# Gate rows fetched into 64 of 128 partitions and copied to the other 64 by ScalarE, in a one-core MetaFormer layer

## The chip, the cores and the metric

The kernel runs on one core of one Trainium2 chip. The metric is the device time of one execution in microseconds (us). A core has TensorE (PE in the profile; PEld is its weight load), VectorE (DVE), ScalarE (ACT), GpSimd (POOL) and SyncE (SP), each with its own instruction queue that is worked off in order; SP here only issues DMAs.

## The reference: what is computed

Input `x` is 2 x 128 x 256 x 256 float32 (batch, channels, rows, columns). All arithmetic is float32.

```
x = x + attention(norm_over_channels(x))        # 8x8 windows, 4 heads, keys and values from 12x12 with a
                                                # mask that keeps positions of the query's own parity
t = tokens(x)                                   # 131072 tokens of 128 channels
h = norm(t)
p = softmax(h @ router_w + router_b)            # 8 experts; the best two kept, renormalised
t = t + sum over the two kept experts of p_e * (h @ expert_w[e] + expert_b[e])
```

Only the second half matters for the change. Each token has eight gate values (six of them zero), a mean and a rate (one over its standard deviation).

## The kernel before

**Work and order.** The image is cut into 64 strips of 8 rows, and a strip into four *planes* by the parity of row and column (the mask lets a query see its own parity only). The loop at L979 runs over 256 planes, each with 512 query positions. In the same iteration the kernel also works on one *row pair* (2 x 256 = 512 tokens) of an earlier strip for the experts. The order of the instructions of every engine is written out by hand (`manual_schedule`, L978): generators (`scores`, `attend`, `project`, `norms`, `route`, `out_project`) are advanced with `next`, so the place of a `next` or a call in the loop is the place of its instructions in the queues.

**One iteration on PE**, in order: position scores (L437), key scores (L454), the next plane's values (L310), position terms (L369), keys (L383) and queries (L408), expert products 4, 6, 7, 5 of the earlier row pair (L677), softmax sums (L475), attention times values (L485), channel sums for the norms (L543), expert products 0, 1, 2 of the next row pair (L677), output projection (L513), product 3 (L677). A matmul of the program stands as two matmul records and two weight loads in the profile.

**The gates.** For a row pair `f` and a row `c` that attention will need, `norms` (L526) makes channel sums on PE; DVE transposes them into `plg` (L552) and works out variances (L192 to L195); ScalarE takes a logarithm and an exponential (L196, L197); DVE goes on with L198. In the next iteration `route` (L569) makes the gates on DVE (L576 to L608). `spread` (L611) transposes gates, means and rates (L614) and writes them to a DRAM tile `gd`, one 512-long row per expert, one for the means (row 8) and one for the rates (row 9). Each such row is then read back by one DMA that repeats it on all 128 partitions:

- `Experts.fetch(e)` (L643) loads gate row `e` into a tile `gb` of 128 x 512. The pool has eight of them. A one-column write by DVE (L651) or ScalarE (L649) stands before the DMA (L652), so that the DMA goes out when that engine has come to this point.
- `fetch_means` (L654) loads the means into `sb` (L657), `fetch_rstd` (L625) the rates into `rb` (L628).
- `means` (L659) makes `xs = x + sb` on DVE (L662; the row holds the standard deviation minus the mean, the former carrying the bias); `times(e)` (L664) makes `xe = xs * gb` on DVE for e = 0, 1, 2, 3, 4, 6 and on POOL for 5 and 7 (L668), where a small copy (L672) holds POOL until DVE has made `xe` 6. `ln1` (L234) multiplies a row of `x` by `rb` on POOL (L236) for the attention norm.

All these DMAs are issued by SP, in the order of the calls, with the loads of `x` (`xt`, L117), the stores of the output (L715), the value rows written to DRAM (`vrows`, L329) and the value windows read back from there (`vwin`, L341).

**ScalarE in one iteration**, in order: the exponential of the router (L581), the exponential of the scores (L462), the values to SBUF (L318), the keys (L394, L404) and queries (L410) to SBUF, two squares (L537), a touch of `xt` (L116), then L196 and L197; the touches for gates 4, 5 and 7 (L649) lie between.

**The instruction stream of PE.** At the start of an iteration with n > 6 a padding instruction (L994) moves the next PE instruction to slot 157 of a block of 256 instruction slots (`BLOCK` = 256, `FIRST_LIMIT` = 99: 99 slots are left in the block). With 64 slots for L437 and two for each record of L454, the block ends at the 18th of the 128 records of L454; 256 slots later is the fourth record of the first L677, and 256 after that the 108th of 128 records of L485. `row_at` (L886) gives the row `c`; it is None for the last seven planes (249 to 255), and such an iteration has 16 matmul records fewer. There `late` (L992) adds a second padding to slot 40 (L1026) ahead of L475.

**The start.** In planes 0 to 5 (`filling`, FILL = 6) no experts are due; `norms` gets a PSUM tile of the experts for its sums (L1034), but takes `plg` from the pool of three PSUM tiles `mm` that `pv`, `pu`, `pk`, `pq` and `po` use in turn.

Of the kernel before, what the change touches and what calls it, by code (L numbers as in the profile page):

```python
# [19 lines left out]
E = 8  # L20
# [32 lines left out]
def kernel(  # L53
# [472 lines left out]
    def norms(f, c, nm, plt=None):  # L526

        g = gboth[next(g_turn) % len(gboth)]
        srcs = []
        for j, src in ((0, f and rows_of(*f)), (2, c and ln1_src(*c))):
            if src is None:
                continue
            sq = work.tile([P, CH], F32, tag=f"sq{j}", name=f"sq{j}{nm}", bufs=1)
            nc.scalar.activation(sq, src, AF.Square)  # L537
            srcs += [(j, src), (j + 1, sq)]
        yield
        plt = plt or mm_tile(f"plt{nm}")  # L540
        for j, src in srcs:
            for t in range(NT):
                nc.tensor.matmul(  # L543
                    plt[32 * t : 32 * t + 32, :P],
                    lhsT=rw[:, j],
                    rhs=src[:, t * P : (t + 1) * P],
                    start=(j == srcs[0][0]),
                    stop=(j == srcs[-1][0]),
                )
        yield  # L550
        plg = mm_tile(f"plg{nm}")
        nc.vector.transpose(plg[:, :P], plt[:, :P])  # L552
        p4 = plg[:, :P].rearrange("p (t e) -> p t e", e=32)
        k0, k1 = (0 if f else 1), (2 if c else 1)
        r, u = rstd(p4, plg[:, P : P + 2 * NT], k0, k1, nm)
        rs = None
        if f:
            rs = small.tile([P, NT], F32, tag="rs", name=f"rs{nm}")
            nc.vector.scalar_tensor_tensor(rs, u[:, 0], 3.0, r[:, 0], ALU.add, ALU.mult)
        if c:  # L560
            nc.vector.scalar_tensor_tensor(
                g[:, 1, :, 1], u[:, 1 - k0], 3.0, r[:, 1 - k0], ALU.add, ALU.mult
            )
        yield g, rs, p4
# [60 lines left out]
    def fetch_rstd(gd, nm):  # L625

        rb = gates.tile([P, NT * P], F32, tag="rb", name=f"rb{nm}", bufs=2)
        nc.sync.dma_start(rb, to_all(gd, E + 1))  # L628
        return rb

    def to_all(gd, j):

        return gd[j * NT : (j + 1) * NT].rearrange("r k -> (r k)").partition_broadcast(P)

    class Experts:

# [6 lines left out]
        def fetch(self, e, eng):  # L643


            nm = "_".join(str(v) for v in (*self.at, e))
            self.gb[e] = gates.tile([P, NT * P], F32, tag="gb", name=f"gb{nm}", bufs=8)
            if eng is nc.scalar:
                eng.copy(self.gb[e][:, 0:1], onesm[:, 0:1])  # L649
            else:  # L650
                eng.memset(self.gb[e][:, 0:1], 0.0)  # L651
            nc.sync.dma_start(self.gb[e], to_all(self.gd, e))  # L652

        def fetch_means(self):  # L654

            self.sb = gates.tile([P, NT * P], F32, tag="sb", name="sb%d_%d" % self.at, bufs=1)
            nc.sync.dma_start(self.sb, to_all(self.gd, E))  # L657

        def means(self):  # L659

# [24 lines left out]

    class NoExperts:
        def fetch(self, e, eng):
            pass

        def fetch_means(self):  # L690
# [31 lines left out]
    def finish_last(ex, nxt, gated):  # L722
# [65 lines left out]
        nxt.means()  # L788
        ex.end()
        for e in (0, 1, 2, 3, 4, 6, 5, 7):  # L790
            nxt.times(e, nc.vector)
        for e in (0, 1, 2, 3, 4, 6, 5, 7):
            nxt.product(e)
# [57 lines left out]
        for r in range(4):  # L851
# [6 lines left out]
        store(*to_store.pop())  # L858

        fetch_into(  # L860
            2, gds[1], [gates.tile([P, CH], F32, tag="gb", name=f"gl2_{e}", bufs=8) for e in range(E)]
        )

        accs = []
# [113 lines left out]
    with tc.manual_schedule(engines={ET.PE, ET.DVE, ET.Activation, ET.Pool, ET.SP}):  # L978
        for n in range(n_planes):  # L979
# [9 lines left out]

            late = n == 6 or n > 6 and row_at(n - 1) is None  # L992
            if n > 6 and (not late or row_at(n - 2) is not None):
                nc.tensor.addr_align(BLOCK, offset=BLOCK - FIRST_LIMIT)  # L994


# [8 lines left out]
            next(score, None)  # L1005
            next(ahead, None)
            nxt.fetch(7, nc.scalar)
            if gated:
                f, c, made = gated
                gd = spread(f, c, made[0], f"_{n}")  # L1010
                new = Experts(*f, gd) if f else new
# [16 lines left out]

            f = (i - 1, pl) if 0 < i <= len(strips) else None
            c = row_at(n)  # L1030
            if f or c:
                room = None
                if filling:
                    room = ps_acc.tile([P, 512], F32, tag="acc", name=f"plt_{n}")  # L1034
                norm = norms(f, c, f"_{n}", room)
            next(norm, None)
            next(attn, None)
            nxt.means()
            new.fetch_means()
            if n + 1 < n_planes:  # L1040
                take_values(n + 1)
            for e in (0, 1, 2, 3):
                nxt.times(e, dve)
            new.fetch(0, dve)
            for e in (4, 6):
                nxt.times(e, dve)
            new.fetch(1, dve)
            ex.end()
            new.fetch(2, dve)
            next(attn, None)  # L1050
# [94 lines left out]
```

## Time and profile before

| | us |
|---|---|
| median of 3 runs | 4280.03 (4274.47 to 4294.36) |
| the profiled execution | 4275.43 |
| its span, first to last instruction | 4273.6 |
| PE busy | 4202.6 (98%) |
| DVE busy | 3785.9 (89%) |
| ACT busy | 1316.4 (31%) |
| POOL busy | 1072.7 (25%) |
| DMA traffic | 1022.15 MB, 239 GB/s on the mean |

How to read the profile: the page gives busy time per engine, DMA traffic per queue, the chain of work that ended last, and groups of instructions by source line with their mean duration. The timeline lists one engine's instructions in order of time: start, duration, engine, line, operation, tiles, shape, count; in square brackets the idle time of the engine before the row and what ended it. "issue" there means that nothing in the profile explains the wait. The view of waits sums the same idle times by who waited for whom: us in total, times, longest. The view of windows gives busy us per engine for a stretch of time, then the granted PE clock, the share of the 16 DMA engines that was busy, and GB/s. "In plane" times below count from the first L437 matmul of an iteration.

### The profile page before, as it was taken

The numbers are of one execution on the slowest core, as the hardware profiler recorded it, in microseconds if no ns is written. First come the engines' busy times: TensorE is split into PE (matmuls) and PEld (weight loads), VectorE is DVE, ScalarE is ACT, GpSimd is POOL, SyncE is SP. The second block draws the span as 40 slices with busy tenths as digits, with TensorE's granted clock in tenths as the row PEclk, the third lists the DMA queues.
The fourth block names the chain that finished last, engine by engine and source line by source line (L and its number), as shares of the span: only waits on it lengthen the run. The fifth ranks groups of instructions, "written<-read, shape, count | busy, mean of one in ns | idle before, by whom it ended". The sixth has DMA issues, their size and how long they took to land.

```text
span 4273.6 us, 224029 instructions
## 1 busy us (share of the span) xinstructions
PE 4202.6 (98%) x94273; PEld 2454.3 (57%) x94273; DVE 3785.9 (89%) x11768; ACT 1316.4 (31%) x3750; POOL 1072.7 (25%) x1109
## 2 busy tenths in 40 slices
PE   7999999999999999999999999999999999999998
PEld 5555555555555555555555555555555555555554
DVE  5898889899888899998989988898989899888888
ACT  3323232323333333333333333232323233323220
POOL 1222222222222222222222222222222222222220
PEclk9999999999999999999999999999999999999999
DMA  4777778787878787887777877788777878787776
GB/s 136 233 243 243 241 244 241 246 245 243 247 237 249 236 247 241 250 240 245 246 245 239 248 241 245 237 249 241 246 242 243 243 245 250 235 239 244 238 223 218
DMA packets 824576, 1022.15 MB, mean 239 GB/s; under 512 B 137634, under 2 KB 409634, under 8 KB 823594
## 3 DMA queue, kind: packets, MB, share of 16 engines
q1 hardware_dynamic: 822864, 1007.52, 76.3%
q8 instruction: 769, 12.60, 1.3%
q14 instruction: 213, 1.74, 0.1%
q10 hardware_dynamic: 730, 0.29, 0.0%
HBM read 863.78 MB, written 143.75 MB: 236 GB/s over the span
## 4 chain that ended last, share of the span: by engine, by line
PE 97%; issue 1%; DVE 1%; DMA 0%; SPq 0%; ACT 0%; DVEq 0%
PE acc L677 41%; PE att L454 8%; PE att L485 7%; PE pv L310 7%; PE plt L543 6%; PE pu L369 5%; PE po L513 5%; PE pk L383 5%; PE pq L408 5%; PE att L437 4%; PE att L475 3%; PE accl L765 0%; DMA gl<-gd_l 0%; DVE xe L668 0%; PE pltn L253 0%
## 5 line engine op out<-in xcount | busy, mean ns | idle before, releaser
L677 PE MATMUL acc<-xe,ew 128*128 128x512 f32 x4016 | 1875.4, 599 | 4.3 <-issue 3.6
L677 PEld LDWEIGHTS acc<-xe,ew 128*128 128x128 f32 x4016 | 741.0, 189 | 900.6 <-issue 849.9
L668 DVE TENSOR_TENSOR xe<-xs,gb 128x512 f32<-128x512 f32 x1508 | 932.4, 685 | 8.6
L672 POOL COPY last<-xe 128x1 f32<-128x1 f32 x250 | 46.5, 186 | 3030.0 <-DVE gb L651 3030.0
L668 POOL TENSOR_TENSOR xe<-xs,gb 128x512 f32<-128x512 f32 x500 | 637.3, 1275 | 1.5 <-PE att L485 1.0
L454 PE MATMUL att<-qs,kcol 32*60 32x32 f32 x32768 | 393.1, 222 | 21.6 <-issue 21.3
L454 PEld LDWEIGHTS att<-qs,kcol 32*60 32x60 f32 x32768 | 387.5, 126 | 26.0 <-issue 25.2
L236 POOL TENSOR_TENSOR xn<-xt,rb 128x512 f32<-128x512 f32 x249 | 374.6, 1505 | 83.6 <-DMA rb<-gd 83.1
L485 PEld LDWEIGHTS att<-pT,vwin 64*32 64x32 f32 x32768 | 351.2, 105 | 49.8 <-issue 12.0
L485 PE MATMUL att<-pT,vwin 64*32 64x32 f32 x32768 | 349.8, 201 | 9.2 <-issue 7.9
L462 ACT ACTIVATE pT<-att 128x1024 f32<-128x1024 f32 x256 | 262.3, 1024 | 265.6 <-PE att L454 265.5
L310 PE MATMUL pv<-wt,xn 128*128 128x128 f32 x2048 | 298.2, 289 | 0.0
L537 ACT ACTIVATE sq<-xt 128x512 f32<-128x512 f32 x501 | 290.1, 630 | 0.0
L357 DVE STREAM_TRANSPOSE au<-auT 128x512 f32<-128x512 f32 x256 | 269.6, 1053 | 8.8
L394 ACT COPY kcol<-pk 128x560 f32<-128x560 f32 (+2 forms) x344 | 183.1, 532 | 290.5 <-PE pk L383 287.7
L373 DVE STREAM_TRANSPOSE uT<-pu 128x512 f32<-128x512 f32 x256 | 183.3, 716 | 96.7 <-PE pu L369 92.3
L513 PE MATMUL po<-o,wt 128*128 128x512 f32 x512 | 262.0, 593 | 4.7 <-ACT kcol L404 2.1
L383 PE MATMUL pk<-xn,wt 128*128 128x512 f32 (+2 forms) x528 | 263.6, 583 | 0.0
L369 PE MATMUL pu<-xn,wrel 128*128 128x512 f32 x512 | 263.3, 596 | 0.0
L408 PE MATMUL pq<-xn,wt 128*128 128x512 f32 x512 | 262.5, 594 | 0.5 <-issue 0.5
L310 PEld LDWEIGHTS pv<-wt,xn 128*128 128x128 f32 x2048 | 249.3, 192 | 10.6 <-DVE xn L236 0.2
L437 PEld LDWEIGHTS att<-au,keys 32*64 32x64 f32 x8192 | 115.8, 131 | 197.1 <-PE po L513 188.5
(2444 smaller groups left out, 4913.5 us busy)
## 6 DMA issues: line engine op xcount, KB each, us to landing
gb<-gd SPq DMA_DIRECT2D x2008, 256.0 KB, 5.7
vwin<-vrows SPq DMA_DIRECT2D x512, 240.0 KB, 4.9
xt<-in_x_dram SPq DMA_DIRECT2D x256, 256.0 KB, 6.6
out_dram<-xt SPq DMA_DIRECT2D x256, 256.0 KB, 6.1
sb<-gd SPq DMA_DIRECT2D x251, 256.0 KB, 4.4
rb<-gd SPq DMA_DIRECT2D x249, 256.0 KB, 3.4
vrows<-vr SPq DMA_DIRECT2D x168, 256.0 KB, 3.6
vrows<-vr SPq DMA_DIRECT2D x160, 128.0 KB, 3.5
```

What stands on the lines that cost most here:

```text
L236: eng.tensor_tensor(xn[i % 2][:, :, :, k, 1 : PC + 1], ln1_src(i, k).rearrange("p (y j x) -> p y x j", y=2, x=2), rb.rearrange("p (y j x) ...
L310: nc.tensor.matmul(pv[:, j * P : (j + 1) * P], lhsT=xp[:, k, 1 : PC + 1], rhs=wv, start=True, stop=True,)
L369: nc.tensor.matmul(pu, lhsT=wrel, rhs=inner, start=True, stop=True)
L383: nc.tensor.matmul(pk[:, : m * PC], lhsT=wk, rhs=xp[:, part[0] : part[0] + m, 1 : PC + 1], start=True, stop=True,)
L408: nc.tensor.matmul(pq, lhsT=wq, rhs=inner, start=True, stop=True)
L437: nc.tensor.matmul(sc[rows, h].rearrange("p (t w z) -> p t w z", w=2, z=16)[:, :, w], lhsT=keys[hp, turn, w], rhs=au[hp, half * NP + w : ( ...
L454: nc.tensor.matmul(sc[rows, h, 32 * t : 32 * t + 32], lhsT=kk[hp, half * HP + t, 0:NK], rhs=qs[hp, m0 : m0 + 2].rearrange("p m a s -> p (m ...
L485: nc.tensor.matmul(av[hp, half, 32 * t : 32 * t + 32], lhsT=vv[rows, t, hp], rhs=pT[rows, h, 32 * t : 32 * t + 32], start=True, stop=True,)
L513: nc.tensor.matmul(po, lhsT=wo, rhs=state["o"].rearrange("p f z -> p (f z)"), start=True, stop=True)
L537: nc.scalar.activation(sq, src, AF.Square)
L668: eng.tensor_tensor(self.xe[e], self.xs, self.gb.pop(e), ALU.mult)
L677: nc.tensor.matmul(self.acc, lhsT=ew[:, e, :], rhs=self.xe.pop(e), start=(e == 0), stop=not self.xe)
```

## The change

1. `fetch`, `fetch_means` and `fetch_rstd` load a row into 64 partitions only: the lower half for an even row number, the upper half for an odd one. A ScalarE copy (`other_half`) then fills the other 64. There are ten such copies in an iteration, at fixed places in ScalarE's order: gate 2 after the values (L318); gates 3, 4, 6 after the queries (L410), ahead of the two squares; means, gate 5, rates, gate 7 and the next row pair's gate 0 between the touch of `xt` (L116) and L196; gate 1 after L197.
2. Ten `gb` tiles instead of eight, and the loads of the next row pair's gates 0 and 1 are issued right after the means, ahead of the `vwin` reads on SP and ahead of the `times` on DVE, where before they stood behind `vwin` and between the `times`.
3. In planes 0 to 5, `plg` takes the other half of the tile that the sums are in, and no tile of `mm`.
4. The conditions for the two paddings of the PE stream are shifted by one plane. They differ from before in planes 249 and 250 alone: 249 now gets the second padding too, 250 loses the first.
5. In `finish_last` the copies stand before the `times` of the row pair that is under way; the loads of the last five row pairs stay at 128 partitions.

```diff
+        room = plt
         plt = plt or mm_tile(f"plt{nm}")
...
-        plg = mm_tile(f"plg{nm}")
+        plg = mm_tile(f"plg{nm}") if room is None else room[:, 2 * P :]
...
-        nc.sync.dma_start(rb, to_all(gd, E + 1))
+        fetch_half(rb, gd, E + 1)
...
+    def to_all(gd, j, count=P):
+        return gd[j * NT : (j + 1) * NT].rearrange("r k -> (r k)").partition_broadcast(count)
+    def halves_of(tile_, j):
+        return (tile_[0:SLOT], tile_[SLOT:])[:: 1 - 2 * (j % 2)]
+    def fetch_half(tile_, gd, j):
+        nc.sync.dma_start(halves_of(tile_, j)[0], to_all(gd, j, SLOT))
+    def other_half(tile_, j):
+        there, other = halves_of(tile_, j)
+        nc.scalar.copy(other, there)
...
-            self.gb[e] = gates.tile([P, NT * P], F32, tag="gb", name=f"gb{nm}", bufs=8)
+            self.gb[e] = gates.tile([P, NT * P], F32, tag="gb", name=f"gb{nm}", bufs=10)
...
-            nc.sync.dma_start(self.gb[e], to_all(self.gd, e))
+            fetch_half(self.gb[e], self.gd, e)
+        def double(self, e):
+            other_half(self.gb[e], e)
...
-            nc.sync.dma_start(self.sb, to_all(self.gd, E))
+            fetch_half(self.sb, self.gd, E)
+        def double_means(self):
+            other_half(self.sb, E)
...
         for e in (0, 1, 2, 3, 4, 6, 5, 7):
+            if e > 1:
+                nxt.double(e)
             nxt.times(e, nc.vector)
...
-            late = n == 6 or n > 6 and row_at(n - 1) is None
-            if n > 6 and (not late or row_at(n - 2) is not None):
+            late = n == 6 or n > 6 and row_at(n) is None
+            if n > 6 and row_at(n - 1) is not None:
                 nc.tensor.addr_align(BLOCK, offset=BLOCK - FIRST_LIMIT)
...
             nxt.fetch(7, nc.scalar)
+            nxt.double(2)
...
             c = row_at(n)
+            for e in (3, 4, 6):
+                nxt.double(e)
...
             new.fetch_means()
+            new.fetch(0, dve)
+            new.fetch(1, dve)
             if n + 1 < n_planes:
                 take_values(n + 1)
-            for e in (0, 1, 2, 3):
+            for e in (0, 1, 2, 3, 4, 6):
                 nxt.times(e, dve)
-            new.fetch(0, dve)
-            for e in (4, 6):
-                nxt.times(e, dve)
-            new.fetch(1, dve)
             ex.end()
...
             new.fetch(3, dve)
+            new.double_means()
+            nxt.double(5)
+            if row:
+                other_half(row[2], E + 1)
+            nxt.double(7)
+            new.double(0)
...
             ex.product(2)
+            new.double(1)
             new.fetch(4, nc.scalar)
```

More of the change, by code (lines that the diff above doesn't have):

```diff
@@ L627, in fetch_rstd @@
         rb = gates.tile([P, NT * P], F32, tag="rb", name=f"rb{nm}", bufs=2)
-        nc.sync.dma_start(rb, to_all(gd, E + 1))
+        fetch_half(rb, gd, E + 1)
         return rb
-    def to_all(gd, j):
-        return gd[j * NT : (j + 1) * NT].rearrange("r k -> (r k)").partition_broadcast(P)
+    def to_all(gd, j, count=P):
[7 more added lines that the diff above has]
+        nc.scalar.copy(other, there)
     class Experts:
@@ L687, in fetch, with double, double_means @@
         def fetch(self, e, eng):
+            pass
+        def double(self, e):
+            pass
+        def double_means(self):
             pass
@@ L860, in finish_last @@
         fetch_into(
-            2, gds[1], [gates.tile([P, CH], F32, tag="gb", name=f"gl2_{e}", bufs=8) for e in range(E)]
+            2, gds[1], [gates.tile([P, CH], F32, tag="gb", name=f"gl2_{e}", bufs=10) for e in range(E)]
         )
```

## The prediction

> **What bounds the kernel now.** First the page: busy time and queues.
>
> ```profile
> PE 4202.6 (98%) x94273; PEld 2454.3 (57%) x94273; DVE 3785.9 (89%) x11768; ACT 1316.4 (31%) x3750; POOL 1072.7 (25%) x1109
> ...
> q1 hardware_dynamic: 822864, 1007.52, 76.3%
> q8 instruction: 769, 12.60, 1.3%
> ```
>
> PE is the bound, and DVE is close behind. q8 moved 769 packets in 256 planes, three for each: 12.60 MB / 769 = 16.4 KB, one block of 256 instruction slots. So PE's program arrives by DMA, beside 1007 MB of data.
>
> Then I took the start of every plane (its first L437) from the timeline. Of the 246 planes from 8 to 253, 141 take 16.24 us to within 0.03; the rest are longer, by 43.8 us in sum. 16.24 is a floor: in such a plane PE is never idle. I looked in the long planes for the difference, line by line. The timeline of PE in planes 230 and 135:
>
> ```profile
> 3778.90 0.36 PE L454 MATMUL att<-qs,kcol 32*60 32x32 f32 x17
> 3780.46 1.31 PE L454 MATMUL att<-qs,kcol 32*60 32x32 f32 x111 [1.20 <-issue]
> ...
> 2226.54 1.45 PE L677 MATMUL acc<-xe,ew 128*128 128x512 f32 x3
> 2228.81 2.31 PE L677 MATMUL acc<-xe,ew 128*128 128x512 f32 x5 [0.82 <-issue]
> ...
> 2231.50 1.16 PE L485 MATMUL att<-pT,vwin 64*32 64x32 f32 x107
> 2232.83 0.32 PE L485 MATMUL att<-pT,vwin 64*32 64x32 f32 x21 [0.17 <-issue]
> ```
>
> The breaks come after 17 records of L454, 3 of L677 and 107 of L485, and no semaphore ends them: these are the three block ends of the layout that L994 makes. Summed over planes 8 to 253 (time of each group of records above its usual one): L454 24.1 us in 48 planes, first L677 8.0 in 20, L485 9.8 in 37; 41.9 in all. I set the q8 packets beside them. A break follows when the packet ends less than about 1.5 us ahead of the block end; without a break it was 1.3 to 4.0 us ahead at L454. The start of that packet in its plane varies from 11.4 to 15.5 us, so it waits its turn among the data.
>
> What it waits behind shows the view of windows, plane 60 in three stretches (0 to 3.5, 3.5 to 12, 12 to 16.25 in plane):
>
> ```profile
> 992.16:995.66 3.50, 3.50 (x171) 3.22 (x171) 3.11 (x16) 1.72 (x4) 0.00 (x0) 1.00 0.92 330
> 995.66:1004.16 8.50, 8.50 (x191) 4.71 (x190) 8.13 (x20) 2.83 (x8) 1.46 (x3) 1.00 0.66 202
> 1004.16:1008.41 4.25, 4.25 (x11) 1.58 (x10) 3.52 (x15) 0.47 (x3) 2.65 (x2) 1.00 0.82 279
> ```
>
> The last two columns are DMA share and GB/s: the DMA engines are nearly full from 12 us to the next plane's 3.5. Over 145 undisturbed planes, 14 to 16 of the 16 are busy there.
>
> **The change, part by part.**
>
> *Half loads.* 2008 + 251 + 249 = 2508 loads of 256 KB, 657 of 1007 MB, are halved: 329 MB less, a third. By the records a 2 KB packet takes 101 ns on the mean; 2508 x 64 fewer on 16 engines are 1.01 ms, so the DMA share goes from 0.76 to about 0.52. Gates 0 and 1 also leave the crowded stretch (issued at 10.8 and 11.3 in plane) for the idle one near 8. I set a backlog for each issue from these times: 0.81 us of work per 256 KB, 0.93 for a `vwin`. Before, it stands at 2 to 2.7 us from 11 to 16; after, at 0.4 to 1.4. Packets for L454 and L677 then start 1 to 2 us earlier, and their breaks should nearly all go. L485's packet starts at 6.1 to 8.2 behind gate 7, `vrows` and `gd`, of which only the first is halved; I leave 3 us there and 1 elsewhere. Bounds: nothing goes (0), all goes (-41.9). I take **-38**, nearer to the full end, because breaks are the tail of the packets' distribution.
>
> [...]
>
> *Ten copies on ScalarE.* The trace has no 64x512 copy from SBUF to SBUF. Nearest: the pair of L537 squares, same length from SBUF, 1.15 us for two, the second starting about 0.52 after the first; alone 0.63. I take 0.52 each in a row; bounds 0.18 (the one-column copy L649) and 0.65 (L394, 128x560): 5.2 us in a plane, ACT from 31% to about 62%. What counts is the queue behind them:
>
> ```profile
> 998.34 1.15 ACT L537 ACTIVATE sq<-xt 128x512 f32<-128x512 f32 x2
> 999.39 0.18 ACT L116 COPY xt<-onesm 128x1 f32<-128x1 f32 x1
> 1006.69 0.18 ACT L196 ACTIVATE r__60_19346<-plg 128x8 f32<-128x8 f32 x1 [7.12 <-DVE plg L195]
> ...
> DVE uT L373 <- PE pu L369: 92.3, 216, 5.5
> ```
>
> - Gate 2: ACT is idle 0.86 us ahead of L394 after the touch at 3.6 to 3.8 in plane; 0.52 fits.
> - Gates 3, 4, 6, from 6.2 to 7.8: their rows landed by 3.4, 4.8 and 5.7 (medians), DVE wants them at 8.6, 9.2 and 9.7. The squares end at 9.1 in place of 7.3; PE reads them from 11.0 (L543). Covered by about 1.5 us.
> - Means, gate 5, rates, gate 7, gate 0, then L196: ACT sits idle for 7.12 us there, until DVE's L195 at 14.52. Before, `sb` landed at 12.6 (issued 8.1, 4.4 on the way). After: `rb` waits for `gd`, which lands earlier with less traffic ahead; I take `sb` issued at 7.6, 3.5 on the way (between `rb`'s 3.4 and its own 4.4), so 11.1; gate 0, issued at 8.0, by 11.8. Five copies end at 13.7: 0.8 us spare. Cost 0. If the cover is gone, L196 is late, then L198 and all of DVE; DVE's own slack is its wait for `pu`, 0.22 us at the median.
> - POOL: gate 5's copy ends near 12.1, so POOL starts some 1.5 us later (10.7 before), ends near 16.1; `xe` 7 is read at 7.3 of the next plane, the `xn` row at 1.9 of the next (18.2). Covered by 3 us or more.
> - SP: as many issues as before; `vwin` goes behind two more issues of 0.4, but it waited until 9 for `vrows` anyway. Gate 4's touch moves behind gate 1's copy, 0.6 later; its row is due 8 us later.
>
> *Ten tiles.* Gate 0 then takes the place of the earlier gate 5, freed by POOL at about 16, where eight tiles would need `times` 0 first. Without this, the early loads could not go out. Cost 0.
>
> *Paddings.* In plane 249 a break of 2.44 stands at 4108.8, and the granted clock is 0.5 for the next 3.4 us, so L454 and L310 take 1.79 where 1.31 and 1.09 are usual: 3.6 together. With the padding in its place the blocks end where they do elsewhere. Of this, L454's 0.5 is in the 41.9 already: **-3**.
>
> *Start.* In planes 0 to 5 PE's L513 waits for ACT's L404, L197 or DVE: 2.1 + 1.3 + 1.2 + 0.2 = 4.8 us by the view of waits, because `po` takes the tile that two others hold. Without `plg` it takes an earlier one: **-3**. Breaks of 2.0, 0.6, 2.9 and 1.3 us in planes 0 to 5 come with hardly any gate traffic, they stay. One of 4.38 in plane 6 lies behind the first eight gate loads; with the half clock after it (L310 and L369 1.8 too long) I count **-2**, bounds 0 and -6. The copies of `rb` and `sb` ahead of L196 can cost 1 to 2 in plane 5, inside the breaks.
>
> *End.* Loads stay whole, PE's path is the same; six copies stand beside eight `times` (4.7 us): 0, within 3 on both sides.
>
> **Sum** against the profiled execution: 4275.4 - 38 - 3 - 3 - 2 = 4229. It is 4.6 below the median of 4280.03; breaks fall differently in every run, and with few left that difference should mostly go too, so I say 4231, within 4208 (all breaks gone, the early ones too) and 4255.
>
> **Rivals.**
>
> - *The packets are not freed* (time near 4267): their delay comes from `xt`, `vwin` and stores, which stay whole, or 64-row loads cost the engines nearly as much as 128-row ones. For it: `vrows` of 128 KB landed in 3.5 us, of 256 KB in 3.6. Against: that is landing time with fixed parts, and the share of 0.92 in the stretch of gates 5, 6 and 7 is theirs. Only -8 for paddings and start remains. With half of the breaks it would be 4250.
> - *ScalarE's queue takes the place of the fetch* (slower): five copies wait for `sb`, L196 waits for them, and DVE for L197. If `sb` lands at 12.6 as before, they end at 15.2, L196 is 0.68 late, 0.22 is slack: 0.46 in each of 248 planes, 114 us; with the gains 4275 - 46 + 114 = 4343. It decides from a lateness of 0.22 + 46/248 = 0.41 on, copies ending at 14.93. Against it: less traffic ahead of `gd`, `rb` and `sb`, and half of their own.
> - *The copies cost far more than 0.52* (0.9 and more) gives the same lateness; I count it in with the second.
>
> **How the numbers follow.** Forecast 4231 with 0.70; packets not freed 0.13 (4250 to 4275, a third of it under 4259); ScalarE's queue 0.17 (4285 to 4345). A measurement of this kernel tells about 0.5% (21 us) from no change. Faster: 0.70 + 0.04 = 0.74. Same: 0.09 + 0.02 = 0.11. Slower: 0.15. The range from 4206 to 4285 takes in the first two cases and leaves out most of the third. The forecast's own range is 4208 to 4255.
>
> **What would show it.** Right: a DMA share near 0.52; planes of 16.24 nearly throughout; "issue" at L454 and L677 under 5 us together; `sb` landing before 12, L196 still waiting for DVE's L195. Wrong: L198 waiting for L197 longer than its 0.48; "DVE uT <- PE pu" near zero; breaks at the block ends as before; a 64x512 copy above 0.65 us.

## The result, and the profile after

The changed kernel takes **4297.02 us** (median of 13 runs, 4291.34 to 4301.75); the kernel before, beside it on the same chips, 4282.43 (13 runs). Ratio 1.0026, 95% interval 1.0016 to 1.0036: slower by about a quarter of a per cent. The forecast was 4231.

From the page of the changed kernel, busy times and the first two queues:

```profile
PE 4253.0 (99%) x94273; PEld 2504.3 (58%) x94273; DVE 3828.4 (89%) x11768; ACT 2837.7 (66%) x6258; POOL 1079.7 (25%) x1109
...
q1 hardware_dynamic: 662352, 678.79, 55.8%
q8 instruction: 769, 12.60, 1.2%
```

The DMA share fell from 76.3% to 55.8%, and PE is *busier*, by 50 us, with the same 94273 matmuls. So the profile shows no more waiting of PE than before: the time is booked inside its instructions. The groups of matmuls by line (before the bar: busy time and mean of one; behind it: idle time ahead of them and what ended it), first of the kernel before, then of the changed one:

```profile
L454 PE MATMUL att<-qs,kcol 32*60 32x32 f32 x32768 | 393.1, 222 | 21.6 <-issue 21.3
...
L485 PE MATMUL att<-pT,vwin 64*32 64x32 f32 x32768 | 349.8, 201 | 9.2 <-issue 7.9
```

```profile
L454 PE MATMUL att<-qs,kcol 32*60 32x32 f32 x32768 | 408.3, 222 | 5.7 <-issue 5.7
L485 PE MATMUL att<-pT,vwin 64*32 64x32 f32 x32768 | 385.0, 200 | 4.6 <-issue 4.3
```

Behind the bar the breaks are gone (21.6 to 5.7, 9.2 to 4.6; the rest lies in the first planes). Ahead of it L454 lasts 15 us longer and L485 35. The mean of one record (222, 200 ns) has not changed: the records overlap, so a record that starts late adds to the busy time of its line and makes no idle time. The timeline of the changed kernel shows it in planes 60, 61 and 64; the same group of 128 matmuls takes three times:

```profile
1006.57 1.69 PE L485 MATMUL att<-pT,vwin 64*32 64x32 f32 x128
...
1023.20 1.50 PE L485 MATMUL att<-pT,vwin 64*32 64x32 f32 x128
...
1072.30 1.34 PE L485 MATMUL att<-pT,vwin 64*32 64x32 f32 x128
```

1.34 is the undisturbed time (with the last record's own length; from first start to the next line's start it is 1.268). In 1.69 the view has no gap: it counts idle time from the end of the record before, and a record lasts 0.2 us, while the next one usually starts some 17 ns after it or sooner. Averaged over planes 10 to 247, sixteen undisturbed records start within 133 ns, and in the changed kernel the third to the sixth sixteen within 149 to 161. The median of these stays at 134, so the records do not run slower throughout. Start by start they keep their pace but for single steps of 80 to 185 ns (5% to 95%) at changing places, which I call *pauses*. In planes 8 to 248, L485 has 222 pauses over 60 ns (beyond the step of 112 that stands behind its 17th record in every plane) in 175 planes; the other 66 planes lose 1.7 us in sum.

The pauses follow the issue of a half load. In plane 60, SP issues two of them (gates 0 and 1) beside L485:

```profile
1006.40 0.47 SPq L642 DMA_DIRECT2D gb<-gd  x1
...
1006.98 0.54 SPq L642 DMA_DIRECT2D gb<-gd  x1
```

The two pauses of that plane end at 1007.26 and 1007.90, 0.86 and 0.92 us after these starts. Of the 222, 219 end 0.78 to 1.0 us after the start of such an issue (5% to 95%: 0.85 to 0.94). L454 has 99 pauses over 60 ns, 87 of them at that distance; they hold about half of its loss, and smaller steps the rest.

For every kernel I took planes 8 to 248 (241 planes), summed for each line its time above the undisturbed one (L454 1.430, L485 1.268 us), and split this *excess* into gaps between records over 0.15 us (breaks) and the rest. As a gap counts from the end of the record before, some 0.2 us of each break, and all shorter pauses, stand in the rest:

| | before | after |
|---|---|---|
| start, up to plane 8 | 138.5 | 139.4 |
| planes 8 to 248 (241 of 16.243 would be 3914.6) | 3954.5 | 3980.0 |
| of it L454: gaps / rest | 15.0 / 7.8 | 0 / 22.3 |
| first products: gaps / rest | 3.6 / 3.4 | 0 / 0.1 |
| L485: gaps / rest | 2.7 / 6.4 | 0 / 39.9 |
| last product: gaps / rest | 0 / 0.4 | 1.9 / 1.3 |
| plane 249 to the end | 180.7 | 177.2 |
| span | 4273.6 | 4296.6 |

The difference of 23.0 us is +0.9 at the start, +25.5 in the planes and -3.5 at the end. The 25.5 are 62.2 lost at the small matmuls (L454, L485) and 3.2 at the last product, less the 39.9 that breaks took before. Before, 141 of the planes 8 to 253 had the floor of 16.24; after, 3 have it, and the median is 16.49.

The three stretches of plane 60 that the prediction showed, in the changed kernel (last columns: granted clock, DMA share, GB/s):

```profile
997.00:1000.50 3.50, 3.50 (x171) 3.20 (x171) 3.15 (x13) 1.63 (x4) 0.67 (x1) 1.00 0.50 133
1000.50:1009.00 8.50, 8.50 (x189) 4.81 (x188) 8.11 (x19) 5.69 (x13) 0.18 (x1) 1.00 0.36 113
1009.00:1013.60 4.60, 4.60 (x22) 1.82 (x11) 3.81 (x17) 3.79 (x9) 3.56 (x3) 1.00 0.96 237
```

The engines are freed where the prediction said, at the plane's start (0.92 to 0.50), but not at its end. Over planes 8 to 248 the share of the first 3.5 us fell from 1.00 to 0.51, and that behind 12 us stayed where it was (0.93 before, 0.94 after). The granted clock is 1.00 in planes 8 to 248 of both kernels, so the lost time is not the clock either.

### The profile page after: what moved, and what is told of

The parts are those of the page before. It is cut to its first block, busy times and chain, and to the rows that moved or that the text cites. A ratio compares the mean times of both kernels' runs of the same rounds, so it can differ in the third digit from the quotient of the medians.

```text
span 4296.6 us, 227065 instructions
## 1 busy us (share of the span) xinstructions
PE 4253.0 (99%) x94273; PEld 2504.3 (58%) x94273; DVE 3828.4 (89%) x11768; ACT 2837.7 (66%) x6258; POOL 1079.7 (25%) x1109
## 3 DMA queue, kind: packets, MB, share of 16 engines
q1 hardware_dynamic: 662352, 678.79, 55.8%
## 4 chain that ended last, share of the span: by engine, by line
PE 97%; DVE 1%; issue 1%; DMA 0%; ACT 0%; SPq 0%; DVEq 0%
PE acc L699 41%; PE att L454 8%; PE att L485 8%; PE pv L310 6%; PE plt L544 6%; PE pk L383 5%; PE pq L408 5%; PE pu L369 5%; PE po L513 5%; PE att L437 4%; PE att L475 3%; PE accl L793 0%; DVE xe L690 0%; DMA gl<-gd_l 0%; PE pltn L253 0%
## 5 line engine op out<-in xcount | busy, mean ns | idle before, releaser
L647 ACT COPY gb<-gb 64x512 f32<-64x512 f32 x2008 | 1212.5, 616 | 37.3 <-DMA gb<-gd 0.7
L647 ACT COPY sb<-sb 64x512 f32<-64x512 f32 x251 | 154.9, 617 | 451.0 <-DMA sb<-gd 372.4
L454 PE MATMUL att<-qs,kcol 32*60 32x32 f32 x32768 | 408.3, 222 | 5.7 <-issue 5.7
L485 PEld LDWEIGHTS att<-pT,vwin 64*32 64x32 f32 x32768 | 381.4, 105 | 50.1 <-issue 5.3
L454 PEld LDWEIGHTS att<-qs,kcol 32*60 32x60 f32 x32768 | 406.2, 126 | 6.5 <-issue 6.0
L236 POOL TENSOR_TENSOR xn<-xt,rb 128x512 f32<-128x512 f32 x249 | 373.6, 1500 | 75.0 <-ACT r__1_864 L196 30.1
L485 PE MATMUL att<-pT,vwin 64*32 64x32 f32 x32768 | 385.0, 200 | 4.6 <-issue 4.3
L582 ACT ACTIVATE lg<-lg 128x32 f32<-128x32 f32 x252 | 57.8, 229 | 359.0 <-DVE lg L581 353.3
```

The lines of the kernel that those rows point to most:

```text
L236: eng.tensor_tensor(xn[i % 2][:, :, :, k, 1 : PC + 1], ln1_src(i, k).rearrange("p (y j x) -> p y x j", y=2, x=2), rb.rearrange("p (y j x) ...
L454: nc.tensor.matmul(sc[rows, h, 32 * t : 32 * t + 32], lhsT=kk[hp, half * HP + t, 0:NK], rhs=qs[hp, m0 : m0 + 2].rearrange("p m a s -> p (m ...
L485: nc.tensor.matmul(av[hp, half, 32 * t : 32 * t + 32], lhsT=vv[rows, t, hp], rhs=pT[rows, h, 32 * t : 32 * t + 32], start=True, stop=True,)
L647: nc.scalar.copy(other, there)
```

## The experiments

Theory A: a load into only 64 partitions slows the small matmuls that run beside it. B: the ScalarE copies do. C: the order puts loads beside L485. Each kernel is the changed one but for what is named, where nothing else is said. A span is that of one profiled execution; where a ratio stands, the kernel ran 4 to 12 times. Times of the kernel before scatter by some 20 us from run to run, so a difference of single spans below that tells little; the excesses by line tell more.

**Half the columns instead of half the partitions** (`columns`): the same bytes and ten copies of half the length; it leaves out gate columns 256 to 511, which become copies of columns 0 to 255 (`NT * P // 2` is 256).

```diff
-        nc.sync.dma_start(halves_of(tile_, j)[0], to_all(gd, j, SLOT))
+        nc.sync.dma_start(tile_[:, 0 : NT * P // 2], to_all(gd, j)[:, 0 : NT * P // 2])
-        nc.scalar.copy(other, there)
+        nc.scalar.copy(tile_[:, NT * P // 2 :], tile_[:, 0 : NT * P // 2])
```

> The changed kernel, with each load taking the first 256 columns to all 128 partitions in place of 512 columns to 64, and ScalarE copying these 256 columns to the other 256: the other half of the gates is left out of the computation. Bytes as in the changed kernel, rows twice as many and half as long. Theory A in the form that the rows packed into 64 partitions matter: L454 and L485 lose under 10 us together, hardly any break, span 4230 to 4250. Theory A in the form that any short load does it: 60 us stay, span 4290 to 4300. Theory B: the copies are shorter (256 columns), so 30 to 60 us stay.

Span 4368.0. L485 is at 1.267 to 1.269 from the 5th to the 95th percentile, excess 0.0: order, bytes and number of copies are those of the changed kernel, so C falls, and B with it but for the copies' length. The time was missed: breaks at L454, 78.7 us in gaps, took the place of the slow records. The timeline of plane 59:

```profile
1001.09 0.36 PE L454 MATMUL att<-qs,kcol 32*60 32x32 f32 x17
1003.11 1.57 PE L454 MATMUL att<-qs,kcol 32*60 32x32 f32 x111 [1.66 <-issue]
...
1013.31 1.34 PE L485 MATMUL att<-pT,vwin 64*32 64x32 f32 x128
```

**Always the lower half** (`lower_only`: `halves_of` without its turn).

> The changed kernel with every row loaded into the lower 64 partitions (no alternation), ScalarE copying upward. Theory A: the same loss if it is the packing as such, span 4290 to 4305; more loss (L454 + L485 80 us and over) if two loads that follow each other into one half hinder each other and PE; less if the upper half is what hurts. Theories B and C: as the changed kernel, 62 us, span 4297.

Span 4285.9, L485 excess 37.3, L454 20.0, both without gaps: which half is loaded does not matter.

**Whole loads, copies kept** (`full_copies`).

> The changed kernel with every gate, mean and rate load filling all 128 partitions again; the ten ScalarE copies stay (they rewrite a half with the same data), and so do the order, the ten tiles and the paddings. In planes 8 to 248 the changed kernel lost 22.3 us in L454 and 39.9 us in L485, spread over the records without a single break. Theory A (loads into 64 partitions slow the small matmuls that run beside them): both go, L485 to under 10 us, L454 to its fetch breaks; breaks with 'issue' come back, 10 to 25 us; span 4255 to 4275. Theory B (the ScalarE copies slow PE): both stay, with breaks on top, span 4300 to 4320. Theory C (the new order puts some load beside L485, whatever its shape): L485 stays near 40, L454 goes, span 4285 to 4305.

Span 4561.8, a badly chosen kernel: each tile now waits for a whole load and then for a copy that writes it again, and the chain of work goes through them (PE 37%, DVE 28%, DMA 19% of it). Only this can be read from it: L485's excess is 5.3 us, with the copies in place. (L454 has 75.9 us of gaps.)

**Gates 2, 3, 5, 7 halved, the rest whole and not copied** (`mixed`).

> The changed kernel with whole loads and no copy for gates 0, 1, 4 and 6, means and rates, whose transfers lie beside L454 and L485; gates 2, 3, 5 and 7 stay halved with their copies. Theory A: L454 and L485 lose under 15 us together, breaks under 10 us, span 4235 to 4255, faster than before by 0.5 to 0.9%. Theory B: four of ten copies are left, so some 25 us stay, span 4255 to 4270. Theory C: L485 stays near 40, span 4270 to 4285.

4615.29, ratio 1.0785 (1.075 to 1.082). L485 is clean (median 1.269), as theory A says, but L454 has 204.2 us of gaps. Something in the order costs more than the change can win; the next kernels name it.

**The kernel before, every load as two of 64 partitions** (`split_before`): order, bytes and ScalarE as before.

```diff
-        nc.sync.dma_start(rb, to_all(gd, E + 1))
+        fetch_whole(rb, gd, E + 1)
...
+    def fetch_whole(tile_, gd, j):
+        for rows in (slice(0, SLOT), slice(SLOT, P)):
+            nc.sync.dma_start(tile_[rows], to_all(gd, j, SLOT))
```

> The kernel before, its order and its eight gate buffers, with each of the ten loads of a plane issued as two loads of 64 partitions (lower, then upper); no ScalarE copies; the bytes are those of before. Theory A (a load into only 64 partitions slows the small matmuls of L454 and L485 that run beside it): the 128 records of L485 take over 1.35 us in the median instead of 1.268 and those of L454 over 1.45 instead of 1.430, without gaps, on top of the breaks at fetch blocks; span 4310 to 4400 us. Rival D (the slow records come from the ScalarE copies or from the new order, which this kernel lacks): L485 1.268 and L454 1.430 outside the breaks, span 4265 to 4300 us.

Span 5211.8, far more than expected: the second issues and landings make the gates late (DVE waits 432 us for `gb`). But the small matmuls answer: L485 median 1.609, 59.7 us of excess beside 36.6 in gaps; L454 median 1.571, 33.3 us, none in gaps. The granted clock is lower in this kernel (0.938 on the mean), but in the 178 planes where L485 runs at a clock of 1.00 and without a gap, its median is 1.546 all the same. Here are no ScalarE copies and not the new order. So loads into 64 partitions are enough for the loss, and B is not needed for it.

**The new order with whole loads, no copies** (`whole_early`).

> The changed kernel (its order, ten gate buffers, paddings) with whole loads into 128 partitions and no ScalarE copies. Theory A: L485 at 1.268 us and L454 at 1.430 outside gaps. Theory E (the loads of gates 0 and 1 put ahead of the window's values make the third fetch packet of a plane start about 2 us later, as it did in the kernel that loaded half the columns): breaks of PE at L454 of 80 to 250 us in all, instead of 15 before; span 4330 to 4600 us. If the order is harmless: breaks as before, span 4260 to 4290 us.

Span 4539.3, L454 gaps 178.5. Theory E holds: with gates 0 and 1 loaded ahead of `vwin`, the third q8 packet of a plane starts at 15.06 us instead of 12.81 before, both medians of the undisturbed planes alone (31 here, 141 before). With half columns it is 14.51. The changed kernel has hardly any undisturbed plane; there the median of all planes is 12.56, against 13.25 before.

**All halves, gates 0 and 1 late again** (`half_late`; their copies go beside gate 2's, in the next plane).

> The changed kernel with all ten half loads, but gates 0 and 1 loaded again where the kernel before loads them (after the window's values) and copied in the next plane beside gate 2; so of the loads into 64 partitions only those of rates and means run beside L485. Theory A: the excess of L485 over 1.268 us falls from 39.9 us to 15 to 35 us, that of L454 stays at 15 to 25 without gaps; span 4270 to 4295 us. Rival C (the new order of the loads is the cause, not the 64 partitions): L485 back to under 5 us of excess, span 4255 to 4265 us.

L485 excess 12.1 (15 to 35 expected), L454 17.2 without gaps; span 4319.8. With gates 0 and 1 gone from its side, L485 loses less, as A says, but its median is undisturbed (1.268; 79 of 241 planes are over 1.30), though rates and means are loaded beside it. The pauses tell why: rates and means are issued 1.4 and 0.8 us ahead of L485 (medians), so that 0.85 us later mostly falls ahead of it or on its first records. Of its 64 pauses 63, and all 52 of L454, end 0.78 to 1.0 us after the start of a half load's issue. The time was missed by 25 us: 45 us of gaps stand behind L544 (17.8) and behind the last product, ahead of the next L437 (27.7). I come to them below.

**Halves only where no small matmul runs beside** (`half_five`: the order of `half_late`; gates 0, 1, 2, 3, 7 halved, the rest whole).

> As the kernel before it in this batch, but only gates 0, 1, 2, 3 and 7, whose loads run beside the large products, are loaded as halves and copied; rates, means and gates 4, 5 and 6, whose loads run beside L485 or L454, are whole and not copied. Theory A: L485 at 1.268 us and L454 at 1.430 outside gaps; breaks at L454 fall from 15 us to 0 to 8, at the first products from 7 to 2 to 6; excess of planes 8 to 248 10 to 25 us instead of 39.9; span 4245 to 4265 us, ratio 0.993 to 0.998. Rival E (any mix of whole and half loads delays the fetch packets as the first mix did): breaks over 60 us at L454, ratio over 1.01.

4268.1, ratio **0.9949** (0.9929 to 0.9969): faster than both kernels. L454 7.6 us in gaps and 2.5 of rest, L485 3.5 and 6.1; planes 28.6 us above the floor (10 to 25 expected) instead of 39.9 (before) and 65.4 (after).

**Gate 5 halved too** (`half_six`).

> As the kernel with gates 0, 1, 2, 3 and 7 halved (ratio 0.9949), and gate 5 halved too: its load is issued 1.1 us into a plane, beside the last third of L454. Theory A: L454 rises a little in the median (1.43 to 1.46 us), breaks at fetch blocks fall below those of that kernel (L454 7.6 us in gaps, the first products 1.9, L485 3.5), excess of planes 8 to 248 between 15 and 35 us instead of 28.6; ratio to before 0.992 to 0.998. Rival: any further half load costs more at L454 than the breaks it takes away: excess over 40 us, ratio over 0.998.

Ratio 0.999 (0.9981 to 1.000), profiled span 4264.7 with 23.2 us of excess. The trace has what theory A expected, the runs hardly confirm a gain (0.992 to 0.998 expected); it is not better than `half_five`.

**The copies alone** (`copies_only`: the kernel before, with ten 64x512 copies of a spare tile at the places of the change).

> The kernel before, with ten ScalarE copies of 64x512 per plane added at the places of the changed kernel, between the halves of a spare tile that nothing else reads or writes; loads and their order are those of before. Theory A (the copies do not slow TensorE): L485 stays at 1.268 us and L454 at 1.430 outside the breaks, span 4265 to 4290 us. Theory B (ScalarE beside them slows the small matmuls): L485 over 1.33 us in the median, span 4295 to 4330 us.

Planes 8 to 248: excess 43.6 against 39.9; L485 and L454 medians 1.268 and 1.432. B is out. The span, 4306.2, was missed for another reason: the start takes 166.6 us instead of 138.5, 16.9 of it one break ahead of L437 at the end of plane 6.

**96 partitions** (`three_quarters`: `half_late` with `tile_[0:96]` loaded and `[0:32]` copied to `[96:]`).

> As the kernel with all ten half loads and gates 0 and 1 loaded late, but each load fills 96 partitions and ScalarE copies 32 partitions (the same number of copies). If the slowing of the small matmuls is graded with the partitions that a load leaves out: L485 excess 3 to 10 us instead of 12.1 and L454 5 to 14 instead of 17.2, outside gaps. If any load into fewer than 128 partitions does it in full: 12 and 17 us as there. If 96 behave like 128: under 2 us at both outside gaps, with breaks at L454 of 2 to 12 us. Span 4290 to 4330 us in all cases, since the copies make the VectorE chain as late as there.

L485 excess 0.2, L454 1.1, not one gap at either, and a single time of 4252.06. 96 partitions behave like 128 at PE, the third of the cases, and the breaks expected with it did not come: a quarter of the bytes less is enough to keep the packets in time. The span of 4290 to 4330 was missed by 40 us: DVE is late less often than in `half_late` (13 us of such gaps instead of 45).

**The change itself with 96 partitions** (`early_96`).

> The changed kernel with one difference: each load fills 96 partitions instead of 64, and ScalarE copies 32 partitions instead of 64 (order, buffers, number and places of the copies, paddings stay). Theory A (the 64-partition loads are the only fault of the change): L485 at 1.268 and L454 at 1.430 us outside gaps, which takes some 40 + 20 us off planes 8 to 248; span 4236 to 4252 us, ratio 0.988 to 0.994. Rival E (this order delays the fetch packets as soon as a load has more bytes than a half): breaks of 20 to 180 us at L454, ratio 1.00 to 1.04.

4330.54, ratio 1.0125 (1.0104 to 1.0147): both answers are half right. L485 is clean (0.6), and L454 has 52.1 us of gaps: the third packet starts at 14.42 against 12.75 (undisturbed planes) in `three_quarters`, which moves the same bytes with gates 0 and 1 behind `vwin`. So the change has two faults: the 64 partitions, and an order that only half loads could bear.

**64 partitions in the middle** (`middle`: rates, means, gates 0 and 1 into partitions 32 to 95).

> The changed kernel, with the loads that run beside L485 (rates, means, gates 0 and 1) put into partitions 32 to 95 instead of a lower or upper half, with the same bytes and rows, and two ScalarE copies of 32 partitions each for them instead of one. If it is the number of partitions of a load that counts: L485 excess 30 to 45 us as in the changed kernel (39.9). If it is that one load fills a block of 64 partitions (0 to 63 or 64 to 127) alone: under 10 us. L454 (18 to 24 us) is not touched. Span 4250 to 4310 us.

L485 excess 56.0, without gaps (median 1.467): a load of 64 partitions slows it here too. L454 has 5.3 instead of the 18 to 24 expected: in these longer planes (17.0 us) the gate loads that went out near the plane's start mostly go out at 1.0 us or later, too late for L454 (0.49 to 1.9) by the 0.85 us of the pauses. (The span, 4450.7, has the cost of four more copies in it.)

**Copies of rates and means behind L197** (`late_96b`: `three_quarters`, gates 5 and 7 copied beside 3, 4 and 6).

> As the kernel with loads of 96 partitions and gates 0 and 1 late (one look: span 4250.3 us, 18 us of it waits for ScalarE ahead of L544 and of the last product), with the copies of gates 5 and 7 moved ahead of the router sums and those of rates and means behind L197, so that no copy stands ahead of L196. If those copies made L196 late: the gaps at L544 and the last product go from 12.5 us to under 3, span 4235 to 4245 us, ratio 0.989 to 0.993. If not: span 4247 to 4255 us, as there.

4520.93, ratio 1.057 (1.0556 to 1.0585): wrong, and instructive. PE has no breaks at block ends, L485 and L454 are clean (0.0 and 4.4); PE waits for DVE instead (157.6 us ahead of the first product behind L544 alone), and DVE's own instructions are longer. The lines of DVE, before (L577, L580) and then `late_96b` (L578, L581); `rb` is here the router's bias and not the tile of the rates:

```profile
L577 DVE TENSOR_TENSOR lg<-lg,rb 128x32 f32<-128x32 f32 x252 | 48.4, 192 | 8.8
...
L580 DVE TENSOR_TENSOR lg<-lg,mx 128x32 f32<-128x32 f32 x252 | 48.3, 192 | 8.8
```

```profile
L578 DVE TENSOR_TENSOR lg<-lg,rb 128x32 f32<-128x32 f32 x252 | 211.4, 839 | 8.8
L581 DVE TENSOR_TENSOR lg<-lg,mx 128x32 f32<-128x32 f32 x252 | 197.3, 783 | 8.8
```

The same operations on 32 columns take four times as long. The timeline of `late_96b` at the end of plane 57 shows what runs beside them, first GpSimd, then DVE:

```profile
1012.15 1.51 POOL L236 TENSOR_TENSOR xn<-xt,rb 128x512 f32<-128x512 f32 x1 [3.70 <-ACT rb L646]
1013.62 1.26 POOL L689 TENSOR_TENSOR xe<-xs,gb 128x512 f32<-128x512 f32 x1
```

```profile
1012.85 0.85 DVE L578 TENSOR_TENSOR lg<-lg,rb 128x32 f32<-128x32 f32 x1
1013.74 0.19 DVE L580 TENSOR_REDUCE mx<-lg 128x4 f32<-128x32 f32 x1
1013.96 0.97 DVE L581 TENSOR_TENSOR lg<-lg,mx 128x32 f32<-128x32 f32 x1
```

L578 begins inside GpSimd's L236 and ends as that ends (1013.66 and 1013.70); L581 begins inside the next product and ends as that ends (1014.88 and 1014.93). L580, which begins inside the same product, keeps its 0.19 (0.186 on the mean, here and before). GpSimd waited 3.70 us for the copy of `rb`, and that moved it onto them. `half_late` had the same in smaller measure: L578 took 0.618 on the mean. The profile puts its gaps behind L544 down to DVE and names nothing for those ahead of L437; in `late_96c` below, where L578 is short again, both are gone.

**Only the copies moved** (`moved_copies`: the changed kernel with gates 5 and 7 copied beside 3, 4 and 6, rates first, means behind L197).

> The changed kernel with only its ScalarE copies moved: gates 5 and 7 are copied right after gates 3, 4 and 6 instead of behind the means, the rates are copied as soon as they land, and the means behind L197. Theory F (in the changed kernel GpSimd's products of gates 5 and 7 and its L236 start later because they wait for these copies, so that they run beside L578, which then takes up to 1.1 us instead of 0.192): L578 back to 0.19 to 0.22 us in the mean from 0.349, the excess at the last product from 3.2 to under 1 us, L485 unchanged at 35 to 45 us of excess; span 4286 to 4296 us. Rival: L578 is slowed by the ScalarE copies themselves: its mean stays over 0.30 us.

L578 is back at 0.192 from 0.349, the last product's excess at 0.1: theory F holds for the cause. The span of 4313.8 does not: L454's excess rose from 22.3 to 47.3 without a gap. Gates 4 and 6 now go out at 0.16 and 0.71 us of a plane, not at 16.0 of the one ahead and 0.08, so the moment 0.85 to 0.94 us later falls well inside L454 (0.49 to 1.9), which has 276 pauses over 60 ns instead of 99. L578 was worth at most the 3.2 us at the last product.

**The two faults and GpSimd mended** (`late_96c`: 96 partitions, gates 0 and 1 late, copies as in `moved_copies`).

```diff
-        nc.sync.dma_start(halves_of(tile_, j)[0], to_all(gd, j, SLOT))
+        nc.sync.dma_start(tile_[0:96], to_all(gd, j, 96))
-        nc.scalar.copy(other, there)
+        nc.scalar.copy(tile_[96:], tile_[0:32])
...
-            nxt.double(2)
+            for e in (0, 1, 2):
+                nxt.double(e)
...
-            for e in (3, 4, 6):
+            for e in (3, 4, 6, 5, 7):
                 nxt.double(e)
```

> As the kernel with loads of 96 partitions and gates 0 and 1 late (one look: span 4250.3 us, no breaks, 18 us of waits at L544 and the last product, L578 at 0.336 us in the mean), with the same moves of the copies as in moved_copies: gates 5 and 7 early, rates when they land, means behind L197. Theory F: GpSimd is done before L578, whose mean is 0.19 to 0.22 us; the waits at L544 and the last product fall to under 3 us; span 4232 to 4242 us, ratio 0.988 to 0.993. Rival: the waits come from L196 being late behind copies: they stay over 10 us, span 4246 to 4256 us.

**4238.37** (6 runs), ratio **0.9924** (0.9906 to 0.9942), faster than both kernels, and the lowest time of all. Planes 8 to 248 hold 2.6 us above the floor; 228 of the planes 8 to 253 take 16.24. Its lines that answer to those of the changed kernel:

```profile
q1 hardware_dynamic: 742608, 843.16, 68.9%
...
L454 PE MATMUL att<-qs,kcol 32*60 32x32 f32 x32768 | 385.8, 222 | 7.3 <-issue 7.3
...
L485 PE MATMUL att<-pT,vwin 64*32 64x32 f32 x32768 | 345.1, 200 | 6.4 <-issue 6.3
```

With 68.9% of the DMA engines' time in use instead of 55.8%, planes 8 to 248 have hardly a break (0.4 us of gaps) and no slow records; the idle time in these lines lies outside them.

The kernels that tell the causes apart, planes 8 to 248 (excess in us as gaps / rest; some 0.2 us of each break stand in the rest, and in `columns` and `early_96` the clock was granted at half for 20.5 us of these planes):

| | 64 partitions beside L485 | gates 0, 1 | L454 | L485 | L485 median |
|---|---|---|---|---|---|
| before | none | late | 15.0 / 7.8 | 2.7 / 6.4 | 1.268 |
| after | rates, means, 0, 1 | early | 0 / 22.3 | 0 / 39.9 | 1.426 |
| `columns` | none | early | 78.7 / 27.4 | 0 / 0 | 1.268 |
| `split_before` | rates, means (twice) | late | 0 / 33.3 | 36.6 / 59.7 | 1.609 |
| `half_late` | rates, means | late | 0 / 17.2 | 0 / 12.1 | 1.268 |
| `early_96` | none | early | 52.1 / 21.8 | 0 / 0.6 | 1.268 |
| `three_quarters` | none | late | 0 / 1.1 | 0 / 0.2 | 1.268 |
| `late_96c` | none | late | 0 / 0.6 | 0.4 / 0.7 | 1.268 |

## Why the prediction was wrong

**Half loads, -38: the step that failed.** Its first half held. The breaks at block ends are gone (22 us of gaps in planes 8 to 248 before; the 1.9 after stand ahead of L437, where no block ends). In every one of these planes the packet for L454 ended at least 1.45 us ahead of the block end. It starts more evenly (5% to 95% of planes 8 to 248: 11.9 to 13.5 us instead of 11.9 to 15.5), but only 0.7 us earlier at the median, and the packet for the first products 1.2, where 1 to 2 was forecast; the 11.4 to 15.5 us of the prediction are those of the undisturbed planes, the latest of all started at 16.7. The share came to 0.558 (0.52 forecast; a 2 KB packet took 108 ns on the mean, not 101), and behind 12 us the engines are as full as before. What the step left out is what the loads do to PE: L454 and L485 lose 62 us, most of it in pauses that follow the issue of 64-partition loads, so the term came out at about +22, and with the last product at +25.5. Of the two bounds given, 0 and -41.9, the time lies outside, on the side that was not considered: the prediction bounded the gain of the half loads and never their price, though a 64-partition gate load did not stand in the trace of before and should have been bounded from both sides.

**Gates 0 and 1 "leave the crowded stretch for the idle one".** This part of the step was wrong by itself: moved ahead of `vwin` they delay the third packet by 1.7 us (`early_96` against `three_quarters`). Half loads hid it. How the order does it, the records of DMA do not show: the engines are full to the plane's end in both, from 12.5 us on in `early_96` and from 11 on in `three_quarters`.

**Ten copies, 0: nearly right.** A 64x512 copy takes 0.616 alone and about 0.59 in a row, not 0.52; ACT is at 66%, not 62%. The copy of the means starts at 11.25 us in plane (median), against a landing forecast at 11.1; the copies end just ahead of L196, which mostly still waits for L195. L198's wait grew to 0.52 on the mean from 0.48. ScalarE's queue, the rival with 0.17, did not decide: with the same copies at the same places and no half loads, `copies_only`, the planes changed by 3.7 us. What I left out of this step is that GpSimd, started later, runs into DVE's L578 (0.192 to 0.349 us). It cost PE about 3 us here (`moved_copies`: last product 3.2 to 0.1), and far more in `late_96b`.

**Paddings, -3: right**, the end is 3.5 shorter, 2.5 of it in plane 249 (18.32 to 15.86).

**Start, -5: wrong**, +0.9. The waits ahead of `po` did shrink (4.8 to 0.6 us), and the break in plane 6 fell from 4.38 to 2.94, but L196 now stands behind copies that wait for `rb` and `sb`. From the changed kernel's waits of DVE:

```profile
DVE plt L198 <- ACT r__5_1838 L197: 4.0, 1, 4.0
...
DVE plt L198 <- ACT r__3_1326 L197: 2.7, 1, 2.7
...
DVE plt L198 <- ACT r__4_1562 L197: 2.4, 1, 2.4
```

The prediction put 1 to 2 us of this in plane 5 alone, inside the breaks.

**The rivals.** The time lies in the range of the second one (4285 to 4345), but by no mechanism that the prediction lists; that it lies there is chance. The sign that should have made me doubt the sum, "planes of 16.24 nearly throughout", was the right one to look at: 3 planes have it. That the mechanism of the breaks was right shows `late_96c`: with 96 partitions and gates 0 and 1 late, 4238.37 stands near the 4231 that was forecast for another kernel.

**Left open.** Why loads into 64 partitions make PE pause and those into 96 do not. Not the half (`lower_only`), not a block of 64 (`middle`), not the bytes (`columns`), not the copies (`copies_only`). The pauses stand at a fixed time after the issue, and SP's issues are longer too: it takes 0.45 us to issue a gate row to 64 partitions, 0.30 to 96 and 0.32 to 128 (medians), and the loads of `x`, whole in both kernels, take it 0.59 instead of 0.44. That speaks for something that the two share, but no run here shows what it is. The runs do not part the 64 partitions from the 64 packets of such a load either; `columns` has 128 packets. A load into 32 + 32 partitions was not tried.

## What to carry to other kernels

Price a new form of transfer by what runs beside it, not only by its bytes: read the durations of the small instructions around the issue of a load, in the groups *ahead* of the idle column, since a slowdown without gaps shows in no wait (L485 here: 39.9 us, none of it in gaps). Then read the starts of the single records: a mean can make a few pauses look like a slower pace (here 149 to 161 ns for sixteen records on the mean, 134 at the median). Freed DMA time is spent or kept by the order of the loads: with 96 partitions, L454 had 52.1 us of gaps with gates 0 and 1 early and none with them late. What must not be late here is the instruction packet (it started at 14.42 us in plane in the former and at 12.75 in the latter, medians of undisturbed planes), so look at what stands ahead of it when it is due. A copy that makes GpSimd start later can lengthen a DVE instruction that had been clear of it, as L578 here (0.192 to 0.349 us on the mean in the changed kernel, 0.839 in `late_96b`).

## What the runs showed of the hardware that I had not expected

- After the issue of a load of 128 KB into 64 partitions, the matmuls of L454 and L485 paused, L485 for 80 to 185 ns a time, 0.85 to 0.94 us after the issue began (5% to 95%). With loads of 192 KB into 96 partitions in the same order (`early_96`) L485 had 0.6 us of excess instead of 39.9, and with 256 KB into 128 partitions (before) its median was 1.268 us instead of 1.426. The eight products that stand together took 3.524 us at the median, before and after. By what the matmuls lose this time to the loads, no run shows.
- DVE's L578, 0.192 us alone, took 0.85 beside GpSimd in plane 57 of `late_96b`, and up to 1.11 in the changed kernel. There, 86 of its 252 took over 0.3 us, and each of these ended 45 to 53 ns after the GpSimd product inside which it began. L505, with two inputs as L578, took 0.691 on the mean before and after, though 247 and 196 of its 256 began inside a GpSimd product; why the one is lengthened and the other not, no run shows.
- One instruction packet of 16 KB per plane that starts 1.7 us later (`early_96` against `three_quarters`, undisturbed planes) goes with 52.1 us of gaps in 241 planes instead of none; 2.25 us later (`whole_early` against before) with 178.5 instead of 15.0.
